# A gated recurrence and a local-attention network on one core: the convolution's taps and the input gate move to PSUM, the squares into the recurrence's tile, and the order is planned anew

## The chip, the cores and the metric

The kernel runs on one core of a Trainium2 chip. The metric is the device time of one execution in microseconds; of several executions the median is given. A core has five queues that run side by side: TensorE (PE, matrix products; its weight loads are shown apart as PEld), VectorE (DVE), ScalarE (ACT), GpSimd (POOL) and SyncE (SP, which only issues transfers here). Data lie in SBUF, products arrive in PSUM. All data are 32-bit floats but for two small constants.

## The reference

Input x is 16 sequences of 512 tokens with 128 channels. Each is normalised (xn), and goes through two branches whose results are multiplied and added to x.

```python
x = L0_attn_x
xn = _layernorm(x, axis=-1)
s = _L0_attn_ref(xn, ...)
g = _silu(_L0_ffn_ref(xn, ...))
x = x + s * g
```

The first branch is the one that the change touches. Its core:

```python
x_conv = _causal_depthwise_conv(x, conv_w, conv_b)      # four taps
r_t = jax.nn.sigmoid(x_conv @ W_r.T + b_r)
i_t = jax.nn.sigmoid(x_conv @ W_i.T + b_i)
a_t = a_base[None, None, :] ** (8.0 * r_t)
inp = i_t * x_conv
scale = jnp.sqrt(jnp.clip(1.0 - a_t * a_t, 0.0))
...
h = a * h + b                                           # over the tokens, b = scale * inp
...
out = out @ W_out.T
rms = jax.lax.rsqrt(jnp.mean(out * out, axis=-1, keepdims=True) + EPS)
return out * rms * gamma
```

The second branch is two layers of local attention (8 heads of 64, windows of 64 tokens that also see the window before; queries and keys are normalised, scaled and rotated) and a gated feed-forward of 341 hidden channels, each with a residual.

## The kernel before

**Tasks and a plan.** The kernel is not written as a loop. `all_work` lists every piece of work as a task: its name, its item (the sequence s, or layer and 128-token tile), its engine, an assumed duration in ns, a due time (`base`, in sequences), the tasks that it comes after, and the tiles that it opens and touches. `schedule` is a list scheduler: it holds assumed times for the five engines, for seven PSUM banks (`BANKS`; the norms have one of their own), each of 128 x 512 numbers, and for each kind of SBUF tile, of which `ROOM` says how many there are. Among the tasks that could start within `REACH` of the earliest, each engine takes the one with the smallest key, and the key is the due time in thousandths plus `TAU[name]`. So `TAU`, one number for each of some 110 task names, sets the order of the instructions in every queue. A change of the form of PE's tiles between neighbouring products (whole array, halves by row or column, quarters) has its assumed price. At the end the tasks are issued in that order, and each engine works its queue in order, waiting only for data and for tiles to come free.

**The task names.** For sequence s, the gates: `ld` loads, `fbn`, `fag`, `fpw`, `fnm` are the first layer norm, `ftx` transposes, `xp` copies to SBUF with room for the convolution's past, `xs0` and `xs1` feed the second branch. `c0` to `c3` are the four taps of the convolution on DVE (`taps`, L594, lines 600 to 604). For the first three sequences (`early`) two of the taps are products on PE instead (`cv`, L590) that `c3` adds. `gr` and `gi` are the gates' products, `sr` and `si` their tanh on ACT (`curve`, L609), `ea` the decay's exponential, `a2`, `m`, `rt` the root, `in` the gated input on DVE (L618), `u` its product with the root on POOL, `sc` the recurrence as one scan on DVE (L905), `yo` the output product, `s2` its squares on ACT (L906), `ms` their sum over channels on DVE (L639), `mp` the inverse root on POOL, `ss` the scaled output on DVE.

For each layer and tile of 128 tokens: `Q`, `K`, `V` are products; on DVE `rq1`, `rq2` (L669, L672) and the same for k multiply by the rotary tables straight from PSUM, and `addq`, `addk` (L676) add the two halves on POOL. ACT squares q and k, `red` (L681) sums the squares on DVE, `n0` to `n9` (L688 to L708) are an inverse root for a pair of tiles in small DVE steps, and `nrm` (L713, POOL) multiplies q and k by it. `tr` (L734, PE) transposes them, ACT copies them out, `sim` (L767, L773) are the scores, `nmA`, `nmB`, `exA`, `exB`, `rA`, `rB`, `PA`, `PB` the softmax (L779, L786, L794, L800), `PT` (L808) transposes the weights, `PV` (L820) mixes the values, `wo` (L838) projects. The feed-forward has `0g`, `0a`, `0ge`, `0hi` (L862), `0yy` and their like for layer 1. `matmul` (L578) is the helper of all large products, so its line stands for many tasks; the tile names in the profile (q, k, v, r, i, 0g, ...) tell them apart.

**Where the pieces lie.** Before, the taps read the padded input in SBUF and add in place to the tile `xc`, in SBUF too. The tanh of both gates goes from PSUM to SBUF (`thr`, `thi`), and `in` works in place on `thi`. The squares have a tile of their own, `s2`. What `u` (POOL) reads stays in SBUF in both kernels.

Of the kernel before, what the change touches and what calls it, by code (L numbers as in the profile page):

```python
# [12 lines left out]
AF = mybir.ActivationFunctionType  # L13
ALU = mybir.AluOpType
AX = mybir.AxisListType
PSUM = bass.MemoryType.PSUM

P = 128
# [6 lines left out]
KCH = 3  # L25
MASKED = -1e30
FIRST_STEP = 0.703952253
ROOT_SCALE = 0.375 * FIRST_STEP
# [6 lines left out]
    "0mv": 4, "1mv": 4, "fmv": 3, "g": 2, "gelu": 3, "h": 1, "hT": 2, "hid": 3, "kT": 4, "lx": 1, "max": 8,  # L35
    "ms": 3, "nx": 2, "oT": 2, "pT": 2, "pr": 3, "qT": 2, "rot": 4, "s": 4, "s2": 1, "sq": 2, "sw": 4, "th": 3,
    "thi": 2, "thr": 2, "vl": 4, "vs": 5, "x": 1, "xS": 5, "xc": 2, "xn0": 1, "xn1": 1, "xnf": 1, "xp": 2,
    "xtok": 2, "y": 3,
}

TAU = {
    "0a": 1332, "0ag": 1361, "0bn": -214, "0g": 295, "0ge": 1013, "0hT": 673, "0hi": -1180, "0nm": 2443,
    "0pw": 1629, "0r0": 999, "0r1": 4747, "0th": 1552, "0tx": 2339, "0yy": 3374, "1a": 1327, "1ag": 2191,
    "1bn": 1403, "1g": -1411, "1ge": -977, "1hT": 340, "1hi": 1571, "1nm": 2027, "1pw": 2179, "1r0": 3590,
    "1r1": -686, "1th": 4228, "1tx": 1647, "1yy": 1623, "K": 726, "PA": 1584, "PB": 1940, "PT": 417, "PV": 4109,
    "Q": 505, "TA": 1016, "TE": -162, "TR": 1100, "V": 1754, "a2": 4566, "addk": 1519, "addq": 648, "c0": 1400,
    "c1": 3192, "c2": 1035, "c3": 1776, "cv": 2050, "ea": 2438, "exA": 5954, "exB": 3760, "fag": -923, "fbn": 3289,
    "fnm": 1563, "fpw": 2230, "ftx": 2290, "gelu": 1287, "gi": 4289, "gr": 410, "in": -183, "kc0": 1034,
    "kc1": 2098, "kz": -827, "ld": 1054, "m": 2, "mp": -177, "ms": 763, "n0": -979, "n1": 1600, "n2": 1473,
    "n3": -1340, "n4": -1193, "n5": -1274, "n6": 1556, "n7": -75, "n8": -378, "n9": 3101, "nmA": 796, "nmB": -228,  # L50
    "nrm": 1410, "oT": 2811, "ot": 1591, "pT0": -1116, "pT1": 484, "qc0": 1520, "qc1": 1632, "rA": 1038, "rB": 714,
    "red": 3396, "rk1": -2269, "rk2": -1499, "rq1": 1107, "rq2": 1278, "rt": 2358, "s2": 1049, "sc": 3858,
    "si": -1114, "sim": -1210, "sqk": 2151, "sqq": 2061, "sr": 1587, "ss": 3359, "tf": -389, "tn": -1187,
    "tr": 103, "u": -1111, "vc": 3977, "vd": 1290, "vz": 3543, "wo": 3209, "xld": 1123, "xp": 1259, "xs0": 2257,
    "xs1": 3783, "y": 2584, "yo": 4491, "z": 1426, "zs": 1146, "zx": 2697,
}
# [4 lines left out]
SWITCH = (110, 115, 100, 97)  # L61
WHOLE, ROWS, QUARTERS, COLUMNS, EITHER = range(5)
TOGETHER = 1
RELOAD = 1450
# [34 lines left out]

def all_work(B, NT, lag=2, lead=1, vdve=(), early=3):  # L100
    w = Work()
# [8 lines left out]
    def gates(s):  # L110
        b = s - lead
        add("ld", s, "SP", 60, b, opens=[("xtok", s)], late=3500)
        ln("f", s, b, ("xtok", s), [("ld", s)])
        add("ftx", s, "PE", 440, b, [("fnm", s)], mode=WHOLE, opens=[("bank", "fx", s), ("xp", s), ("xS", s)], touches=[("xnf", s)])
        add("xp", s, "ACT", 480, b, [("ftx", s)], touches=[("xp", s), ("bank", "fx", s)])
        add("xs0", s, "ACT", 480, b, [("ftx", s)], touches=[("xS", s), ("bank", "fx", s)])
        add("xs1", s, "POOL", 1050, b, [("xp", s), ("xs0", s)], touches=[("xp", s), ("xS", s)])
        add("c0", s, "DVE", 800, b, [("xp", s)], opens=[("xc", s)], touches=[("xp", s)])
        on_pe = s < early
        for k in (1,) if on_pe else (1, 2, 3):  # L120
            add(f"c{k}", s, "DVE", 1100, b, [(f"c{k-1}", s)], touches=[("xp", s), ("xc", s)])
        if on_pe:
            add("cv", s, "PE", 1714, b, [("xp", s)], opens=[("bank", "cv", s)], touches=[("xp", s)])
            add("c3", s, "DVE", 670, b, [("c1", s), ("cv", s)], touches=[("bank", "cv", s), ("xc", s)])
        for g, t in (("r", "tr_"), ("i", "ti_")):
            add("g" + g, s, "PE", 857, b, [("c3", s)], opens=[("bank", g, s), ("th" + g, s)], touches=[("xc", s)])
            add("s" + g, s, "ACT", 600, b, [("g" + g, s)], touches=[("bank", g, s), ("th" + g, s)], table=EXP | GELU)
        add("ea", s, "ACT", 620, b, [("sr", s)], touches=[("thr", s)], table=EXP)
        add("in", s, "DVE", 670, b, [("si", s)], touches=[("thi", s), ("xc", s)])
        add("a2", s, "POOL", 1250, b, [("ea", s)], touches=[("thr", s)], opens=[("g", s)])  # L130
        add("m", s, "DVE", 340, b, [("a2", s)], touches=[("g", s)])
        add("rt", s, "ACT", 600, b, [("m", s)], touches=[("g", s)], table=ROOT)
        add("u", s, "POOL", 1250, b, [("rt", s), ("in", s)], touches=[("g", s), ("thi", s)])
        add("sc", s, "DVE", 1930, b, [("u", s)], touches=[("thr", s), ("thi", s)], opens=[("h", s)])
        add("yo", s, "PE", 872, b, [("sc", s)], touches=[("h", s)], opens=[("bank", "yo", s), ("s2", s), ("s", s)])
        add("s2", s, "ACT", 480, b, [("yo", s)], touches=[("bank", "yo", s), ("s2", s)])
        add("ms", s, "DVE", 620, b, [("s2", s)], touches=[("s2", s)], opens=[("ms", s)])
        add("mp", s, "POOL", 1255, b, [("ms", s)], touches=[("ms", s)])
        add("ss", s, "DVE", 1060, b, [("mp", s)], touches=[("ms", s), ("bank", "yo", s), ("s", s)])

    def attention(l, m):
# [26 lines left out]
        for j, n in enumerate(T):  # L168
            B_ = lambda nm, *k: ("bank", nm, *n, *k)
            one = n[1] % NT == 0  # L170
            before = (l, n[1] - 1)
            add("nrm", n, "POOL", 1950, b + j / 4, [("n9", M), ("addq", n), ("addk", n)], touches=[("y", *M), ("rot", *n)])
            if j == 0:
# [8 lines left out]
            for h in "AB":  # L182
                add("nm" + h, n, "DVE", 603, b + j / 4, [("sim", n)], touches=[B_("s" + h)], opens=[("max", *n, h)])
                add("ex" + h, n, "ACT", 1380, b + j / 4, [("nm" + h, n)], touches=[B_("s" + h), ("max", *n, h), ("pr", *n)], table=EXP)
                add("r" + h, n, "DVE", 95, b + j / 4, [("ex" + h, n)], touches=[("pr", *n)])
                add("P" + h, n, "POOL", 1035, b + j / 4, [("r" + h, n)], touches=[("pr", *n)])
            add("PT", n, "PE", 546, b + j / 4, [("PA", n), ("PB", n)], opens=[B_("p0"), B_("p1"), ("pT", *n)], touches=[("pr", *n)], mode=ROWS)
# [194 lines left out]
def gated_recurrence_kernel(ctx: ExitStack, tc: tile.TileContext, a: dict, out: bass.AP):  # L382
# [108 lines left out]
    def cast_masks():  # L491
# [15 lines left out]
    shapes = {  # L507
        "xtok": [P, NT, D], "xc": [P, L], "thr": [P, L], "thi": [P, L], "g": [P, L], "h": [P, L], "s2": [P, NT, D],
        "ms": [P, NT], "s": [P, NT, D], "rot": [P, 2, HEADS, DH], "sq": [P, 2, INNER], "sw": [P, HEADS, DH],
# [84 lines left out]
    def taps(s, i):  # L594

        v, xc = at["xp", s], at["xc", s]
        k = (i + 2) % 4
        v, w = v[:, k : k + L], c["cols"][:, k : k + 1]
        if i == 0:
            nc.vector.tensor_scalar(xc, v, w, c["conv_b"], ALU.mult, ALU.add)  # L600
        elif ("bank", "cv", s) in at and i == 3:
            nc.vector.tensor_tensor(xc, at["bank", "cv", s], xc, ALU.add)
        else:
            nc.vector.scalar_tensor_tensor(xc, v, w, xc, ALU.mult, ALU.add)

    def curve(s, g):

        i = "ri".index(g)
        nc.scalar.activation(at["th" + g, s], at["bank", g, s], AF.Tanh, scale=0.5, bias=half_b[:, i : i + 1])  # L609

# [5 lines left out]
    def gated(s):  # L616
        t = at["thi", s]
        nc.vector.scalar_tensor_tensor(t, t, 1.0, at["xc", s], ALU.add, ALU.mult)  # L618

# [16 lines left out]
    def mean_square(s, i):  # L636
        ms = at["ms", s]
        if i == 0:
            nc.vector.tensor_reduce(ms, at["s2", s], AX.X, ALU.add)  # L639
            return  # L640
        nc.gpsimd.tensor_scalar(ms, ms, 1.0 / D, 1e-6, ALU.mult, ALU.add)
        nc.gpsimd.tensor_tensor(ms, ms, mhalf[:, 0:NT], ALU.pow)
# [248 lines left out]
    def store(s):  # L891
# [13 lines left out]
        "sc": lambda s: nc.vector.tensor_tensor_scan(at["h", s], at["thr", s], at["thi", s], 0.0, ALU.mult, ALU.add),  # L905
        "yo": recurrent, "s2": lambda s: nc.scalar.activation(at["s2", s], tok(at["bank", "yo", s]), AF.Square),  # L906
        "ms": lambda s: mean_square(s, 0), "mp": lambda s: mean_square(s, 1), "ss": scaled,
# [111 lines left out]
```

## Time and profile before

| | |
|---|---|
| median of 3 runs | 1363.07 us (1361.11 to 1366.63) |
| profiled execution, its time | 1364.39 us |
| profiled execution, first to last instruction (span) | 1362.6 us |
| mean granted TensorE clock | 0.98 |
| busy: PE, DVE, ACT, POOL | 1287.0, 1131.4, 1152.6, 1069.5 us |
| busiest DVE group: `red` (L681) | 155.7 us, 128 of 1216 ns |
| taps on DVE (L604) | 65.0 us, 42 of 1547 ns |
| first tap (L600) | 10.3 us, 16 of 641 ns |
| gated input (L618) | 11.6 us, 16 of 728 ns |
| tanh of the input gate, of the other (L609) | 13.1 us, 11.1 us, 16 each |
| squares (L906), their sum (L639) | 9.9 us, 11.0 us, 16 each |
| table loads on ACT | 53 of 1283 ns |

The span is counted on the trace of one execution; busy times overlap between engines, and an engine's idle time costs only where PE, the fullest, waits for it. DVE's mean of 1547 ns for a tap hides two kinds of taps, which the range of durations shows.

### The profile page before, as it was taken

To read this page: it belongs to the slowest core of one execution; us is meant where nothing else is said; L and a number is where in the kernel's file an instruction comes from. 1 tells how busy PE (TensorE), PEld (TensorE's weight loads), DVE (VectorE), ACT (ScalarE), POOL (GpSimd) and SP (SyncE) were. 2 spreads that over 40 slices of the span, in tenths; PEclk is the share of its full clock that TensorE was granted. 3 is DMA by queue.
4 is the path that set the end of the run, shared out by engine and by line. 5 is a ranking of instruction groups with operands and counts; after the bars stand their busy time and mean duration, and the time that the engine had idled before them with its cause. 6 is when DMAs were issued, how large, how long until landed. Compare 5 with 4: busy or idle time off the path is not lost.

```text
span 1362.6 us, 43814 instructions
## 1 busy us (share of the span) xinstructions
PE 1287.0 (94%) x17162; PEld 724.3 (53%) x17162; DVE 1131.4 (83%) x2752; ACT 1152.6 (85%) x3703; POOL 1069.5 (78%) x1009
## 2 busy tenths in 40 slices
PE   6689899999999999999999999999999999999985
PEld 2355456555555555555555555555455555656453
DVE  6888889888998888899898988989888888877752
ACT  5698899888899888899888889988888898889672
POOL 6796989697896878889797988978788787868461
PEclk9799999999999999999999999999999999999988
DMA  6011011111111101111111111111111110112100
GB/s 199 5 45 30 16 23 28 28 41 33 37 33 28 48 18 49 32 37 33 29 37 29 49 33 37 33 29 29 28 37 37 29 33 25 34 29 58 28 21 24
DMA packets 46766, 49.43 MB, mean 36 GB/s; under 512 B 4704, under 2 KB 31456, under 8 KB 46560
## 3 DMA queue, kind: packets, MB, share of 16 engines
q1 hardware_dynamic: 46560, 46.63, 13.7%
q8 instruction: 136, 2.23, 0.7%
q14 instruction: 70, 0.57, 0.1%
HBM read 13.05 MB, written 4.19 MB: 13 GB/s over the span
## 4 chain that ended last, share of the span: by engine, by line
PE 66%; DVE 18%; issue 5%; ACT 5%; POOL 5%; DMA 0%; POOLq 0%; DVEq 0%; ACTq 0%
PE q L578 6%; PE k L578 6%; PE sA L773 5%; PE v L578 5%; PE o L820 5%; PE x L838 4%; PE t L734 4%; DVE norms L681 3%; PE p L808 3%; PE 0g L578 3%; PE 0y L578 3%; PE 0a L578 3%; PE 1a L578 3%; PE 1g L578 3%; DVE sw L672 3%
## 5 line engine op out<-in xcount | busy, mean ns | idle before, releaser
L676 POOL TENSOR_TENSOR rot<-rot,sw 128x512 f32<-128x512 f32 x256 | 326.8, 1283 | 79.3 <-DVE sw L672 68.1
L800 POOL TENSOR_TENSOR pr<-pr,sum 128x512 f32<-128x512 f32 x256 | 267.0, 1052 | 95.1 <-DVE sum L794 89.9
L713 POOL TENSOR_TENSOR rot<-rot,y 128x1024 f32<-128x1024 f32 x128 | 268.2, 2118 | 18.3 <-DVE y L708 18.2
L786 ACT ACTIVATE pr<-sB,max 128x128 f32<-128x128 f32 x512 | 187.4, 423 | 8.6 <-DVE max L779 7.3
L786 ACT ACTIVATE pr<-sA,max 128x128 f32<-128x128 f32 x512 | 192.1, 467 | 0.0
L681 DVE TENSOR_REDUCE norms<-sq 128x16 f32<-128x1024 f32 x128 | 155.7, 1216 | 3.7 <-ACT sq L662 1.3
L811 ACT COPY pT<-p 128x512 f32<-128x512 f32 x256 | 144.2, 658 | 8.1 <-PE p L808 8.1
L786 ACT ACTIVATION_READ_ACCUMULATOR pr<-sA,max 128x1 f32 x512 | 150.7, 306 | 0.0
L669 DVE TENSOR_TENSOR rot<-q,table 128x512 f32<-128x512 f32 x128 | 87.5, 684 | 57.6 <-PE q L578 36.1
L578 PE MATMUL q<-wqkv,xS 128*64 128x512 f32 (+1 forms) x502 | 134.2, 618 | 0.2 <-ACT pr L786 0.2
L773 PE MATMUL sA<-kT,qT 64*64 64x128 f32 x2048 | 133.9, 270 | 0.0
L773 PE MATMUL sB<-kT,qT 64*64 64x128 f32 x2048 | 133.6, 270 | 0.0
L578 PE MATMUL k<-wqkv,xS 128*64 128x512 f32 (+1 forms) x476 | 132.2, 601 | 0.4 <-ACT pr L786 0.3
L743 ACT COPY kT<-t 128x256 f32<-128x256 f32 x256 | 100.6, 434 | 34.9 <-PE t L734 34.4
L820 PE MATMUL o<-pT,vl 128*64 128x64 f32 x2048 | 128.3, 226 | 0.9 <-ACT pT L811 0.9
L786 ACT ACTIVATION_READ_ACCUMULATOR pr<-sB,max 128x1 f32 x512 | 128.2, 261 | 0.0
L578 PE MATMUL v<-wqkv,xS 128*64 128x512 f32 (+1 forms) x500 | 127.2, 603 | 0.7 <-ACT pr L786 0.7
L820 PE MATMUL o<-pT,vs 128*64 128x64 f32 x2048 | 125.7, 224 | 0.2
L838 PE MATMUL x<-oT,wo 128*64 128x257 f32 x1024 | 122.7, 381 | 2.8 <-ACT oT L828 2.3
L773 PEld LDWEIGHTS sA<-kT,qT 64*64 64x64 f32 x2048 | 120.3, 133 | 9.2 <-issue 0.2
L820 PEld LDWEIGHTS o<-pT,vl 128*64 128x64 f32 x2048 | 107.1, 139 | 31.7 <-ACT pT L811 12.2
L773 PEld LDWEIGHTS sB<-kT,qT 64*64 64x64 f32 x2048 | 120.2, 133 | 0.0
(152 smaller groups left out, 3195.7 us busy)
## 6 DMA issues: line engine op xcount, KB each, us to landing
vl<-vs SPq DMA_DIRECT2D x224, 128.0 KB, 2.3
xtok<-in_x SPq DMA_DIRECT2D x16, 256.0 KB, 3.2
x<-in_x SPq DMA_DIRECT2D x16, 256.0 KB, 3.1
out<-th SPq DMA_DIRECT2D x16, 256.0 KB, 2.3
wqkv<-in_wqkv SPq DMA_DIRECT2D x2, 768.0 KB, 7.1
w<-in_w SPq DMA_DIRECT2D x2, 384.0 KB, 6.6
rot<-in_rope SPq DMA_DIRECT2D x1, 512.0 KB, 6.2
wo<-in_wo SPq DMA_DIRECT2D x2, 256.0 KB, 5.3
```

The costliest lines, as they stand in the source:

```text
L578: nc.tensor.matmul(ps[col : col + step], w[:, col : col + step], v, start=start, stop=stop)
L669: nc.vector.tensor_tensor(at["rot", *n][:, i], src, tab, ALU.mult)
L676: nc.gpsimd.tensor_tensor(r, r, at["sw", *n, "qk"[i]], ALU.add)
L681: nc.vector.tensor_reduce(at["nx", *pair(n)][:, 0, 16 * j : 16 * j + 16], sq, AX.X, ALU.add)
L713: nc.gpsimd.tensor_tensor(flat, flat, bc(at["y", *pair(n)][:, 0, 16 * j : 16 * j + 16], DH), ALU.mult)
L743: nc.scalar.copy(at["kT", *pair(n)][:, :, col : col + 64], four(at["bank", f"t{w}", *n])[:, 1])
L773: nc.tensor.matmul(out_(w, par)[:, p, :], q[r, p, half[w]], k[r, p, col : col + P], start=False, stop=p == 3)
L786: nc.scalar.activation(at["pr", *n][:, g, :], sim[:, p, :], AF.Exp, bias=at["max", *n, h][:, p : p + 1], accum_out=at["sum", *n][:, g : g ...
L800: nc.gpsimd.tensor_tensor(w, w, bc(at["sum", *n][:, g], P), ALU.mult)
L811: nc.scalar.copy(at["pT", *n][:, w], heads(at["bank", f"p{w}", *n]))
L820: nc.tensor.matmul(o[64 * par : 64 * par + 64, p, 64 * w : 64 * w + 64], at[("vl", "vs")[w], *n][:, h * DH : (h + 1) * DH], pT[:, w, 4 * p ...
L838: nc.tensor.matmul(ps[64 * r : 64 * r + 64, 0 : 2 * P + 1], w, o[:, k, 1 - r : 2 * P + 2 - r], start=k == 0, stop=k == 3)
```

## The change

The changed parts are these. (1) From the fourth sequence on, the taps are summed in a PSUM bank: `c0` opens it, `c1` and `c2` add in place, `c3` reads it and writes `xc` in SBUF. In the first three sequences `c0` writes `xc`, `c1` adds its tap in place to the bank that holds PE's two taps, and `c3` adds bank and `xc`. (2) The input gate's tanh is written in place in its bank; `in` reads it from there and opens `thi`. (3) The squares go to the tile `h`, whose contents the output product has read by then; `s2` as a tile is gone. (4) The assumed durations of some tasks are changed, all of `TAU` is replaced, and two constants are named: `EARLY`, 3 as before, and `SKEW`, which is 0 and so adds nothing.

```diff
-    "ms": 3, "nx": 2, "oT": 2, "pT": 2, "pr": 3, "qT": 2, "rot": 4, "s": 4, "s2": 1, "sq": 2, "sw": 4, "th": 3,
...
+    "ms": 3, "nx": 2, "oT": 2, "pT": 2, "pr": 3, "qT": 2, "rot": 4, "s": 4, "sq": 2, "sw": 4, "th": 3, "thi": 2,
...
-    "0a": 1332, "0ag": 1361, "0bn": -214, "0g": 295, "0ge": 1013, "0hT": 673, "0hi": -1180, "0nm": 2443,
...
+    "0a": -186, "0ag": 4568, "0bn": 2786, "0g": 1865, "0ge": 1058, "0hT": -1527, "0hi": -1865, "0nm": -2283,
...
-        add("c0", s, "DVE", 800, b, [("xp", s)], opens=[("xc", s)], touches=[("xp", s)])
-        on_pe = s < early
-        for k in (1,) if on_pe else (1, 2, 3):
-            add(f"c{k}", s, "DVE", 1100, b, [(f"c{k-1}", s)], touches=[("xp", s), ("xc", s)])
+        b += round(SKEW * (B - 1 - s) / max(B - 1, 1), 3)
+        on_pe, C = s < early, ("bank", "cv", s)
         if on_pe:
-            add("cv", s, "PE", 1714, b, [("xp", s)], opens=[("bank", "cv", s)], touches=[("xp", s)])
-            add("c3", s, "DVE", 670, b, [("c1", s), ("cv", s)], touches=[("bank", "cv", s), ("xc", s)])
-        for g, t in (("r", "tr_"), ("i", "ti_")):
-            add("g" + g, s, "PE", 857, b, [("c3", s)], opens=[("bank", g, s), ("th" + g, s)], touches=[("xc", s)])
-            add("s" + g, s, "ACT", 600, b, [("g" + g, s)], touches=[("bank", g, s), ("th" + g, s)], table=EXP | GELU)
+            add("c0", s, "DVE", 700, b, [("xp", s)], opens=[("xc", s)], touches=[("xp", s)])
+            add("cv", s, "PE", 1714, b, [("xp", s)], opens=[C], touches=[("xp", s)])
+            add("c1", s, "DVE", 660, b, [("cv", s)], touches=[("xp", s), C])
+            add("c3", s, "DVE", 660, b, [("c0", s), ("c1", s)], touches=[C, ("xc", s)])
+        else:
+            add("c0", s, "DVE", 600, b, [("xp", s)], opens=[C], touches=[("xp", s)])
+            for k in (1, 2, 3):
+                add(f"c{k}", s, "DVE", 660, b, [(f"c{k-1}", s)], opens=[("xc", s)] if k == 3 else [], touches=[("xp", s), C])
+        for g in "ri":
+            add("g" + g, s, "PE", 857, b, [("c3", s)], opens=[("bank", g, s)] + [("thr", s)] * (g == "r"), touches=[("xc", s)])
+            add("s" + g, s, "ACT", 600, b, [("g" + g, s)], touches=[("bank", g, s)] + [("thr", s)] * (g == "r"), table=EXP | GELU)
...
-        add("in", s, "DVE", 670, b, [("si", s)], touches=[("thi", s), ("xc", s)])
+        add("in", s, "DVE", 660, b, [("si", s)], opens=[("thi", s)], touches=[("bank", "i", s), ("xc", s)])
...
-        add("s2", s, "ACT", 480, b, [("yo", s)], touches=[("bank", "yo", s), ("s2", s)])
-        add("ms", s, "DVE", 620, b, [("s2", s)], touches=[("s2", s)], opens=[("ms", s)])
+        add("s2", s, "ACT", 480, b, [("yo", s)], touches=[("bank", "yo", s), ("h", s)])
+        add("ms", s, "DVE", 600, b, [("s2", s)], touches=[("h", s)], opens=[("ms", s)])
...
-            add("nrm", n, "POOL", 1950, b + j / 4, [("n9", M), ("addq", n), ("addk", n)], touches=[("y", *M), ("rot", *n)])
+            add("nrm", n, "POOL", 1880, b + j / 4, [("n9", M), ("addq", n), ("addk", n)], touches=[("y", *M), ("rot", *n)])
...
-                add("P" + h, n, "POOL", 1035, b + j / 4, [("r" + h, n)], touches=[("pr", *n)])
+                add("P" + h, n, "POOL", 1010, b + j / 4, [("r" + h, n)], touches=[("pr", *n)])
...
-        v, xc = at["xp", s], at["xc", s]
+        v, c_ps = at["xp", s], at["bank", "cv", s] if ("bank", "cv", s) in at else None
...
-            nc.vector.tensor_scalar(xc, v, w, c["conv_b"], ALU.mult, ALU.add)
-        elif ("bank", "cv", s) in at and i == 3:
-            nc.vector.tensor_tensor(xc, at["bank", "cv", s], xc, ALU.add)
+            nc.vector.tensor_scalar(at["xc", s] if ("xc", s) in at else c_ps, v, w, c["conv_b"], ALU.mult, ALU.add)
+        elif i == 3 and s < EARLY:
+            nc.vector.tensor_tensor(at["xc", s], c_ps, at["xc", s], ALU.add)
         else:
-            nc.vector.scalar_tensor_tensor(xc, v, w, xc, ALU.mult, ALU.add)
+            nc.vector.scalar_tensor_tensor(at["xc", s] if i == 3 else c_ps, v, w, c_ps, ALU.mult, ALU.add)
...
-        i = "ri".index(g)
-        nc.scalar.activation(at["th" + g, s], at["bank", g, s], AF.Tanh, scale=0.5, bias=half_b[:, i : i + 1])
+        i, ps = "ri".index(g), at["bank", g, s]
+        nc.scalar.activation(ps if i else at["thr", s], ps, AF.Tanh, scale=0.5, bias=half_b[:, i : i + 1])
...
-        t = at["thi", s]
-        nc.vector.scalar_tensor_tensor(t, t, 1.0, at["xc", s], ALU.add, ALU.mult)
+        nc.vector.scalar_tensor_tensor(at["thi", s], at["bank", "i", s], 1.0, at["xc", s], ALU.add, ALU.mult)
...
-            nc.vector.tensor_reduce(ms, at["s2", s], AX.X, ALU.add)
+            nc.vector.tensor_reduce(ms, tok(at["h", s]), AX.X, ALU.add)
...
-        "yo": recurrent, "s2": lambda s: nc.scalar.activation(at["s2", s], tok(at["bank", "yo", s]), AF.Square),
+        "yo": recurrent, "s2": lambda s: nc.scalar.activation(tok(at["h", s]), tok(at["bank", "yo", s]), AF.Square),
```

## The prediction

> **What bounds the kernel now.** I read the page's slices first, then TensorE's waits, then windows of 40 us, then the timelines of one stall.
>
> ```profile
> PE   6689899999999999999999999999999999999985
> ...
> PEclk9799999999999999999999999999999999999988
> ```
>
> Each digit is the busy share of 34 us, in tenths. TensorE (PE) is full from slice 6 to slice 38; only the edges have room. VectorE (83%), ScalarE (85%) and GpSimd (78%) matter only where they make PE wait. The view of PE's waits (what waited, for what: us in total, times, longest) says where that is:
>
> ```profile
> PE t L734 <- POOL rot L713: 25.5, 28, 1.1
> PE fx L568 <- ACT xnf L558: 12.1, 2, 11.6
> PE r L578 <- DVE xc L602: 6.7, 1, 6.7
> ```
>
> The second is the start (first load, first layer norm), the third a prologue wait. The first is the middle: 21.1 us of it, in 22 waits, lie between 160 and 1160 us. The windows show it as a beat (us, busy time of PE, PEld, DVE, ACT, POOL, then granted clock, DMA share, GB/s):
>
> ```profile
> 440.00:480.00 40.00, 38.09 (x556) 22.91 (x554) 36.14 (x105) 35.00 (x117) 35.00 (x35) 0.96 0.18 45
> ...
> 720.00:760.00 40.00, 40.00 (x508) 21.09 (x506) 33.41 (x61) 35.26 (x113) 30.71 (x27) 1.00 0.11 28
> 760.00:800.00 40.00, 38.09 (x579) 23.12 (x576) 37.42 (x112) 36.47 (x120) 36.17 (x36) 1.00 0.17 42
> ```
>
> A period (one sequence through everything) is two windows: 79.77 us from one "0g" group on PE to the next (639.41 to 719.17 us in the chain of waits). 1.9 us of it is idle. The timelines of POOL, DVE and PE at that place (start, length, idle before and releaser):
>
> ```profile
> 764.43 8.92 POOL L713 TENSOR_TENSOR rot<-rot,y 128x1024 f32<-128x1024 f32 x4 [0.89 <-DVE y L708]
> ```
>
> ```profile
> 764.36 3.05 DVE L604 SCALAR_TENSOR_TENSOR xc<-xp,cols,xc 128x512 f32<-128x512 f32 x2
> 767.33 0.41 DVE L845 TENSOR_TENSOR xS<-x,xS 128x257 f32<-128x257 f32 x1
> 767.67 2.05 DVE L604 SCALAR_TENSOR_TENSOR xc<-xp,cols,xc 128x512 f32<-128x512 f32 x1
> ```
>
> ```profile
> 766.92 0.71 PE L734 MATMUL t<-squares,rot 64*128 64x64 f32 x16 [0.81 <-POOL rot L713]
> 767.47 0.66 PE L808 MATMUL p<-squares,pr 64*128 64x64 f32 x16
> 769.22 0.71 PE L734 MATMUL t<-squares,rot 64*128 64x64 f32 x16 [1.10 <-POOL rot L713]
> ```
>
> PE waits twice for GpSimd's normalisations (L713), and these run beside exactly the three convolution taps (L604) that the change rewrites. Forms by line (duration min/median/max):
>
> ```profile
> L604 DVE SCALAR_TENSOR_TENSOR xc<-xp,cols,xc x42: 714/2050/2360, 16.1 to 1087.0; 128x512 f32<-128x512 f32 x42
> L862 DVE SCALAR_TENSOR_TENSOR hid<-0a,cols,gelu x48: 718/749/752, 109.0 to 1265.4; 128x512 f32<-128x512 f32 x48
> L713 POOL TENSOR_TENSOR rot<-rot,y x128: 1892/1905/2831, 43.4 to 1305.8; 128x1024 f32<-128x1024 f32 x128
> ```
>
> A tap reads two tensors in SBUF. Alone it takes 714 ns, beside GpSimd 2050 and more, and GpSimd stretches too: the first L713 here took 2.44 us against its median 1.905. The same operation with one tensor in PSUM (L862) never left 718 to 752 in 48 runs.
>
> **The taps.** From the fourth sequence on (13 sequences) c0 writes a bank, c1 and c2 read and write it, c3 reads it and writes SBUF. In-place PSUM at this size is not in the trace; the nearest row is L862, 749 ns, with a PSUM source. Bounds are 714 (the free tap) and 762 (L862 plus 13, by which small operations that write the norms in PSUM, L694 at 198, exceed those that write y in SBUF, L702 at 185); I take 749. Here the three taps took 0.74, 2.27 and 2.05, 5.06 us; then 3 x 0.749 = 2.25. c0 (L600, median 516 ns) loses its SBUF destination: between 516 and 750, taken 680 as for the PSUM-reading L669. DVE gains 2.81 - 0.16 = 2.65 us in each such period.
>
> [...]
>
> **What that gives PE, in the old order.** Without stretch L713 ends at 764.43 + 1.905 = 766.33 instead of 766.87, and the second at about 768.2 instead of 769.1 (back to back they follow at 1.87). The first transpose comes 0.5 us earlier; the second, behind the 0.55 of p, about 1.0 earlier. So 1.9 us of idle becomes 0.9. The long taps (two of 2.05 or more) recur in the steady periods, sequences 5 to 15, so 11 x 1.0 = 11 us. What is late next is the same L713, released by the inverse norm (y, L708), which is a chain on DVE and no longer helped by faster taps.
>
> **The clock.** Four periods are longer: "0g" starts at 397.02, 478.25, 559.64 and 639.41 us, so 81.23 and 81.39 where 79.77 is usual. In 2 us windows the clock falls to about 0.5 at 286 to 290, 446 to 452, 528 to 534 and 1088 to 1092 us. The two stalls lie 47.8 and 50.1 us behind a period's "0g" (766.92 and 769.22 less 719.17), so at 445 and 447, at 526 and 528: each drop follows that period's stalls. About 1.6 us each, four times: 6.3 us. Shorter stalls should spare them; bounds 0 and 6.3, taken 6.
>
> **The input gate.** si (L609) writes its bank in place, `in` (L618, 728 ns mean) reads it: 749 by L862, 16 x 0.02 = 0.3 us on DVE. ScalarE's row for si is 858 median to SBUF against 687 for sr; a PSUM destination lies between 687 and 858, worth 0 to 2.7 us on an engine with 15% free. Taken 0. The bank is let go after `in`, not after si: 718.14 + 0.86 to 719.52 + 0.69 in one period, 1.2 us later.
>
> **Squares in the recurrence's tile.** Same instructions (L906, L639), another address: nothing. h now lives until `ms`; with one h, the next scan waits for it. Scans are a period apart, scan to `ms` 6 us (1202.7 to 1208.8). Cover: 70 us.
>
> **Early sequences.** Three keep two taps on PE (12 matmuls either way). c1 no longer adds to xc but to the bank: it now waits for PE's `cv`, and behind it on DVE stands whatever is queued. Before, c1 took 0.77, 0.99 and 2.36 us; then 0.75 each, 1.9 us less on DVE. c3's 6.7 us wait at 43.12 starts with a GpSimd table and 0.69 + 0.99 + 0.69 of taps, so 0.3 us of it goes. Taken 0.
>
> **The new order.** All priorities change, on every queue, SP's loads too (DMA share 0.1 in the middle: nothing). PE's instructions stay the same in kind and number. I counted 34 changes of the matmul tiling per period; a group of 16 transposes alone takes 0.64 us to the next start (725.43 to 726.07), two together 1.14, so a change costs some 0.07 to 0.1 us, and three more or fewer move 13 periods by up to 4 us either way. The 1.0 us of idle that the old order would keep is what a new order can hide, since one group of q, k or v (0.86 us) put ahead of the transpose covers it: 11 x 0.9 = 10 us at most, taken 4. It can lose as much elsewhere; its cost bounds are those of the rivals.
>
> Sum against the profiled execution (span 1362.6, time 1364.4): 11 + 6 + 4 = 21, giving 1343.4. It lies 1.3 above the median of the runs, 1363.07; the forecast is 1342. Within this case: 1357 if nothing but half the stall goes, 1332 if all stalls and clock drops go (21.1 + 6.3 and 4 of tiling).
>
> **Rivals.**
> Also the edges: PE is idle 32 us before 160 us, of which 12 are the first load, and at clock 0.83 and 0.91 between 40 and 120 us (some 10 us). If the replan fills a third of both, 10 us, on top of the 31: 1322. For it: every engine has gaps there. Against: chains of one sequence set them.
> No change: the idle is an artefact of order and only moves. PE works 77.9 of 79.77 us; a stall of 1.9 in another place costs the same: 1363. For it: the inverse norm, not the tap, releases L713. Against: GpSimd gets 1.4 us back (8.92 to 7.5) just there.
> Slower, the bank: seven PSUM banks serve all of PE's groups, and c0 must find a free one, standing at the head of DVE's queue until it does. In the traced period c0 to c3 lasts from 760.43 to 769.72, 9.3 us; with the gate's 1.2 that is 10.5 us of one bank. A period has 7 x 79.77 = 558 bank-us, so 1.9% are gone. If banks are what paces PE, that is 1.5 us per period, 13 x 1.5 = 19 us, with the gain lost: 1382. It decides above about 1.6 us per period (21 / 13). [...] For it: PE's weight loads wait for bank readers (o for ACT's pT 12.9 us, v for ACT's pr 10.0). Against: PE itself lost 0.7 us to ACT's pr on v; and taps back to back hold a bank 2.9 us, a 0.5 us price, 7 us in all.
> That the change doesn't do what it says: c0 picks its target by whether xc is open yet, which holds from the fourth sequence on only until c3; I give this nothing of its own.
>
> **Chances.** Forecast 0.52, edges too 0.11, no change 0.10, slower 0.27: planned orders rest on assumed durations, so I don't trust the replan further than that. Half a per cent is about what a measurement tells from no change. Faster 0.63, same 0.10, slower 0.27. The range 1324 to 1384 takes in the bank's case and most of the edges'; the forecast's own is 1332 to 1357.
>
> **What would show it.** Taps of 714 to 762 ns with no long ones; L713 back at 1.9 us; t waiting for L713 under 12 us in total; clock 1.00 in the middle windows; a period near 78.5. Wrong if the period stays at 79.8 with PE waiting on ACT or DVE instead, if c0 shows idle time before it for a bank, or if the middle gains and the edges give it back.

## The result and the profile after

The changed kernel takes 1370.70 us (median of 8 runs, 1369.44 to 1372.20) beside 1365.26 us of the kernel before (8 runs, 1360.53 to 1366.83). The ratio is 1.0048 with a 95% interval of 1.0033 to 1.0063: slower by half a per cent, where 1.6% faster was forecast. The profiled execution has a span of 1370.3 us (before 1362.6). Executions of the kernel before spread from 1357.8 to 1367.7 us over all sessions, with granted clocks from 0.983 to 0.977, and their medians from 1360.5 to 1365.8, so ratios of different sessions can differ by some 0.4%.

The forms by line of the changed kernel (durations min/median/max) show that the operations did what they should:

```profile
L605 DVE TENSOR_SCALAR cv<-xp,cols x13: 783/802/806, 57.9 to 1091.9; 128x512 f32<-128x512 f32 x13
...
L609 DVE SCALAR_TENSOR_TENSOR cv<-xp,cols,cv x29: 733/754/756, 17.8 to 1093.7; 128x512 f32<-128x512 f32 x29
L609 DVE SCALAR_TENSOR_TENSOR xc<-xp,cols,cv x13: 747/748/748, 60.3 to 1094.5; 128x512 f32<-128x512 f32 x13
```

No tap of L609 takes 2 us any more; all lie between 733 and 756 ns. Only the first tap into a bank (`c0`, L605) costs more than assumed, 802 ns. VectorE's busy time fell from 1131.4 to 1107.6 us, GpSimd's from 1069.5 to 1047.5. Yet PE now waits elsewhere. The page's rows for PE and its clock, and the view of PE's waits (what waited, for what: us in total, times, longest):

```profile
PE   5889899999999999999999999999999999999985
...
PEclk9899999999999999999999999999999999999998
```

```profile
PE t L738 <- POOL rot L717: 17.9, 16, 1.6
PE fx L573 <- ACT xnf L563: 11.6, 1, 11.6
PE 0th L573 <- DVE xn L567: 6.8, 11, 0.6
PE i L583 <- DVE sum L798: 6.1, 9, 0.7
```

The wait for the normalisation is smaller in total (25.5 before), but it is one long one per period now, and two waits are new: 0.6 us for a layer norm (11 times) and 0.7 us of the input gate's product (9 times). The timelines of POOL, DVE and PE at the place that corresponds to the one shown of the kernel before:

```profile
683.21 7.48 POOL L717 TENSOR_TENSOR rot<-rot,y 128x1024 f32<-128x1024 f32 x4 [3.57 <-DVE y L712]
```

```profile
679.11 0.43 DVE L692 TENSOR_SCALAR norms<-norms 128x32 f32<-128x32 f32 x2
...
682.87 0.29 DVE L712 SCALAR_TENSOR_TENSOR y<-norms,y 128x32 f32<-128x32 f32 x2
683.08 0.80 DVE L605 TENSOR_SCALAR cv<-xp,cols 128x512 f32<-128x512 f32 x1
683.91 0.76 DVE L609 SCALAR_TENSOR_TENSOR cv<-xp,cols,cv 128x512 f32<-128x512 f32 x1
684.58 0.42 DVE L849 TENSOR_TENSOR xS<-x,xS 128x257 f32<-128x257 f32 x1
684.91 0.74 DVE L609 SCALAR_TENSOR_TENSOR cv<-xp,cols,cv 128x512 f32<-128x512 f32 x1
685.69 0.75 DVE L609 SCALAR_TENSOR_TENSOR xc<-xp,cols,cv 128x512 f32<-128x512 f32 x1
```

```profile
685.16 0.72 PE L738 MATMUL t<-squares,rot 64*128 64x64 f32 x16 [1.26 <-POOL rot L717]
686.59 1.08 PE L583 MATMUL i<-xc,squares 128*64 128x512 f32 x4 [0.71 <-DVE sum L798]
687.47 1.06 PE L583 MATMUL r<-xc,squares 128*64 128x512 f32 x4
```

The inverse norm (L692 to L712, two chains side by side) ends at 683.16. Four normalisations take 7.48 us beside four taps, where they took 8.92. But GpSimd stood idle for 3.57 us before them, waiting for that inverse norm, and PE arrives at the transpose 1.26 us too early all the same. Then it runs into the gate's products, which the new order puts right behind the last tap: the tap ends at 686.44, `i` starts at 686.59. (The view names the reciprocal next in DVE's queue as releaser; `i` reads xc, whose last tap ends just ahead of it.) Before, only `r` followed the last tap, and `i` came 27 us later (769.87 and 796.82 us in that trace).

From one layer-norm product of layer 0 to the next (0th on PE), ten steady periods last 820.8 us here (306.6 to 1127.4), 82.1 each, against 802.6 us, 80.3 each, before. A period is 81.11 us, or 82.7 in the six of the ten in which PE falls to half clock for 3.4 us about the end of the second wait (a clock episode in what follows); before, it was 79.77, or 81.2 to 81.6 with an episode.

### The profile page after: what moved, and what is told of

The parts are those of the page before. It is cut to its first block, busy times and chain, and to the rows that moved or that the text cites. A ratio compares the mean times of both kernels' runs of the same rounds, so it can differ in the third digit from the quotient of the medians.

```text
span 1370.3 us, 43462 instructions
## 1 busy us (share of the span) xinstructions
PE 1292.5 (94%) x16894; PEld 729.3 (53%) x16894; DVE 1107.6 (81%) x2752; ACT 1154.9 (84%) x3703; POOL 1047.5 (76%) x1009
## 4 chain that ended last, share of the span: by engine, by line
PE 49%; DVE 22%; ACT 20%; issue 4%; POOL 4%; DMA 0%; POOLq 0%; ACTq 0%; DVEq 0%
ACT pr L790 10%; PE q L583 5%; DVE norms L685 5%; PE o L824 4%; PE t L738 3%; PE k L583 3%; ACT sq L666 3%; PE 1a L583 3%; PE sA L777 3%; PE 0y L583 3%; PE 1y L583 3%; PE 1g L583 3%; PE 0g L583 3%; PE 0a L583 3%; POOL rot L717 3%
## 5 line engine op out<-in xcount | busy, mean ns | idle before, releaser
L717 POOL TENSOR_TENSOR rot<-rot,y 128x1024 f32<-128x1024 f32 x128 | 253.0, 1996 | 49.5 <-DVE y L712 49.5
L790 ACT ACTIVATE pr<-sB,max 128x128 f32<-128x128 f32 x512 | 183.7, 400 | 23.2 <-DVE max L783 21.0
L790 ACT ACTIVATE pr<-sA,max 128x128 f32<-128x128 f32 x512 | 187.0, 431 | 0.0
L790 ACT ACTIVATION_READ_ACCUMULATOR pr<-sA,max 128x1 f32 x512 | 137.4, 271 | 0.0
L583 PE MATMUL k<-wqkv,xS 128*64 128x512 f32 (+1 forms) x498 | 129.2, 603 | 1.2 <-ACT pr L790 1.2
L790 ACT ACTIVATION_READ_ACCUMULATOR pr<-sB,max 128x1 f32 x512 | 121.8, 239 | 0.0
L738 PEld LDWEIGHTS t<-squares,rot 64*128 64x128 f32 x2048 | 75.0, 140 | 71.9 <-POOL rot L717 33.4
```

The costliest lines, as they stand in the source:

```text
L583: nc.tensor.matmul(ps[col : col + step], w[:, col : col + step], v, start=start, stop=stop)
L717: nc.gpsimd.tensor_tensor(flat, flat, bc(at["y", *pair(n)][:, 0, 16 * j : 16 * j + 16], DH), ALU.mult)
L738: nc.tensor.transpose(four(at["bank", f"t{w}", *n])[:, i, p, :], r[rows, i, 2 * p : 2 * p + 2, :], c["ident"][rows, rows])
L790: nc.scalar.activation(at["pr", *n][:, g, :], sim[:, p, :], AF.Exp, bias=at["max", *n, h][:, p : p + 1], accum_out=at["sum", *n][:, g : g ...
```

## The experiments

In each of them the order of every queue is fixed: the plan of one of the two kernels is made first, each queue's list of tasks is taken from it, and the scheduler may only take the next task of that list, so that it does no more than give out the banks. Comments in the code excerpts are added here. Ratios are to the kernel before, run on the same chip. In the traces PE's groups come in the same order in the kernel before and in both old-order runs that move no product, and where nothing is moved a fixed order lasts as long as the plan it copies: 79.88 and 89.61 us from the second to the fourth `0th` in the last new-order run below, 79.87 and 89.59 in the changed kernel.

### The new operations in the old order

```diff
-    order = schedule(work, TAU, ROOM)
+    other = all_work_other(B, NT)                  # the tasks of the kernel before
+    fixed = sequences(other, schedule(other, TAU_OTHER, ROOM_OTHER))
+    order = schedule(work, TAU_OTHER, ROOM, fixed)
```

> All new operations (taps and input gate in PSUM, squares in h), but every queue's order is that of the kernel before. Theory A (the operations gain, the new order loses): 12 to 21 us under the kernel before, so about 1345 to 1353; GpSimd's four normalisations in a row 7.5 us instead of 8.9, the transposes' wait for them 1 us per period instead of 1.9, fewer half-clock episodes. Theory B (the bank that the taps hold slows PE): 1365 or more, up to 1382, with PE or its weight loads waiting on readers of banks. Theory C (the taps don't matter to PE at all, only the order does): within 3 us of the kernel before.

Measured: 1346.16 us against 1360.53, ratio 0.9888 (0.9873 to 0.9903). Its timelines of POOL and PE at the same place:

```profile
673.18 7.49 POOL L917 TENSOR_TENSOR rot<-rot,y 128x1024 f32<-128x1024 f32 x4 [1.36 <-DVE y L912]
```

```profile
675.14 0.71 PE L938 MATMUL t<-squares,rot 64*128 64x64 f32 x16 [0.54 <-POOL rot L917]
...
677.00 0.71 PE L938 MATMUL t<-squares,rot 64*128 64x64 f32 x16 [0.66 <-POOL rot L917]
```

The two waits of 0.81 and 1.10 us are now 0.54 and 0.66; in all, PE waits 17.3 us for the normalisations where it waited 25.5:

```profile
PE t L938 <- POOL rot L917: 17.3, 28, 1.1
```

The clock, too, is full in the middle (windows: us, busy of PE, PEld, DVE, ACT, POOL, clock, DMA share, GB/s); each steady period is 79.06 to 79.08 us, none is longer:

```profile
640.00:680.00 40.00, 38.80 (x576) 23.01 (x574) 32.59 (x80) 35.77 (x116) 29.18 (x27) 1.00 0.14 38
680.00:720.00 40.00, 40.00 (x522) 21.95 (x517) 36.48 (x94) 35.78 (x117) 36.85 (x37) 1.00 0.16 37
720.00:760.00 40.00, 38.81 (x564) 22.41 (x563) 32.62 (x81) 36.25 (x117) 29.12 (x28) 1.00 0.12 33
```

Theory A holds; the bank (theory B) falls, since here the taps hold a bank for 6.7 us (668.93 to 675.64) and PE is faster, and so does theory C. So the operations win 1.1%, and the new order loses 1.6% (1.0048 / 0.9888 = 1.016; without the reference, 1370.70 / 1346.16, it is 1.8%).

### The new order with taps in SBUF

```diff
-            add("c0", ..., opens=[C], touches=[("xp", s)])
+            add("c0", ..., opens=[("xc", s)], touches=[("xp", s)])
...
-            nc.vector.scalar_tensor_tensor(at["xc", s] if i == 3 else c_ps, v, w, c_ps, ALU.mult, ALU.add)
+            to = at["xc", s] if s >= EARLY else c_ps
+            nc.vector.scalar_tensor_tensor(to, v, w, to, ALU.mult, ALU.add)
```

> The changed kernel in its own order, but from the fourth sequence on the taps are summed in SBUF again. Theory A: slower than the changed kernel by 5 to 20 us (1376 to 1390), since the taps again lie beside GpSimd's normalisations and stretch them. Theory B: faster than the changed kernel, under 1368. Theory C: within 3 us of 1371.

Measured: 1429.05 us, ratio 1.0495 (1.0479 to 1.0511), some 4.4% above the changed kernel. Theory A had the sign, but the size was far above its 20 us. The taps' form and PE at that place say why:

```profile
L812 DVE SCALAR_TENSOR_TENSOR xc<-xp,cols,xc x39: 741/2051/2292, 56.3 to 1146.1; 128x512 f32<-128x512 f32 x39
```

```profile
792.34 0.71 PE L941 MATMUL t<-squares,rot 64*128 64x64 f32 x16 [1.55 <-POOL rot L920]
797.59 1.98 PE L785 MATMUL i<-xc,squares 128*64 128x512 f32 x4 [4.54 <-DVE sum L1001]
```

What was 0.71 us before `i` is 4.54, 3.8 us more, close to the 3 x 1.3 us by which the three taps are longer; and `i` itself takes 1.98 us in place of 1.08, at half clock. The new order leaves no slack between the last tap and the gates' products: it is an order for short taps only, and with long ones it costs PE nearly their full excess and a clock episode in every one of the ten periods (6.8 us or more each, between 359 and 1154 us).

### Only the taps, in the old order

The kernel before in its own order; c0 to c2 of the fourth and later sequences write the bank, all else is as before.

```diff
-        v, xc = at["xp", s], at["xc", s]
+        v, xc = at["xp", s], at["xc", s] if ("xc", s) in at else at["bank", "cv", s]
...
-            nc.vector.scalar_tensor_tensor(xc, v, w, xc, ALU.mult, ALU.add)
+            nc.vector.scalar_tensor_tensor(xc, v, w, xc if s < 3 else at["bank", "cv", s], ALU.mult, ALU.add)
```

> The kernel before in its own order, only the taps of the fourth and later sequences summed in PSUM; gate, squares and early sequences as before. Theory A: within 3 us of the run with all new operations in the old order, since the gate and the squares are worth nothing. If the bank held by the input gate costs something, this is faster than that run by more than 3 us. Theory C: as the kernel before.

Measured: 1347.36 us, ratio 0.9896 (0.9880 to 0.9913), 1.2 us from the run with all operations and inside its interval. The gate in PSUM, the squares in h and the early taps are worth nothing that these runs can tell.

### One product moved in the old order

The task list of PE is edited in 11 periods. One more buffer of rot is needed, since the query's tile is opened ahead of the transpose that frees one; a th buffer makes room for it.

```diff
-    "rot": 4, ... "th": 3,
+    "rot": 5, ... "th": 2,
...
+    q = fixed[0]                                    # PE's list
+    for k in [k for k, t in enumerate(q) if t[0] == "gr"]:
+        if [t[0] for t in q[k - 4 : k + 2]] == ["PV", "tr", "PT", "tr", "gr", "Q"]:
+            q.insert(k - 3, q.pop(k + 1))           # Q ahead of the first tr
```

> The new operations in the old order, and in 11 periods the first query product is put ahead of the two transposes that still wait 1.2 us per period; one more buffer for rot so that it may start, one less for th. If a wait of PE is worth its length: up to 0.86 us in each of 11 periods, 4 to 9 us under the old-order run without the edit, ratio to the kernel before about 0.982 to 0.986. If the wait only moves (the query's bank or its readers come later): ratio 0.988 to 0.991, as without the edit.

Measured: 1331.31 us against 1364.15, ratio 0.9779 (0.9748 to 0.9810), the best of all, and more than the 4 to 9 us that were expected. PE's wait for the normalisation in this run:

```profile
PE t L942 <- POOL rot L921: 9.3, 18, 1.1
```

It is 9.3 us in all (17.3 without the edit), 0.4 per period in the middle where it was 1.2; a period is 78.10 us, 0.97 less than 79.07. Ten of them give 9.7 us of the 14 us between the two profiled spans (1344.1 and 1330.1). Another 4.7 lie ahead of the fourth `0th` (302.9 against 307.5 us), and only 1.2 of these in an edited period. The other 3.4 come where nothing was moved, by the traces mostly from the fifth rot buffer: in the old-order run without the edit DVE finds none free at the start, until GpSimd has read the raw rotary table out of one (`table`, L694).

```profile
35.62 0.69 DVE L873 TENSOR_TENSOR rot<-q,table 128x512 f32<-128x512 f32 x1 [5.00 <-POOL table L694]
```

With five buffers DVE does not wait there, and PE's wait for the first sequences' taps (`r`) falls from 5.8 to 2.0 us. No run has the buffers without the moved product, so the two are told apart by their places in the traces alone.

### One product moved in the new order, at two places

Ahead of the transpose (with the same two buffers changed):

```diff
+    q = fixed[0]
+    for k in [k for k, t in enumerate(q) if t[0] == "gi"]:
+        if [t[0] for t in q[k - 1 : k + 3]] == ["tr", "gi", "gr", "Q"]:
+            q.insert(k - 1, q.pop(k + 2))           # Q ahead of tr
```

> The changed kernel in its own order, but in 10 periods (the seventh to the last sequence) the query product that follows the gates' products is put ahead of the transpose that waits 1.26 us; one more rot buffer, one less th. Theory D (what the new order loses is this one place: 2.0 us of waits per period, and the half-clock episode that follows it in every second period, 0.8 us per period): 0.9 to 1.7 us less per period, 9 to 17 us under the changed kernel, ratio to the kernel before 0.992 to 0.998. Theory E (the loss is spread over tiling changes, banks and smaller waits, so that the moved product only shifts a wait): within 4 us of the changed kernel, ratio 1.002 to 1.008.

Or between the transpose and the gates' products (buffers as in the changed kernel):

```diff
-            q.insert(k - 1, q.pop(k + 2))
+            q.insert(k, q.pop(k + 2))               # tr, Q, gi, gr
```

> The changed kernel in its own order, but in the same 10 periods the query product stands between the transpose and the gates' products, so that it covers the 0.71 us wait for the last tap. No buffer is changed. Theory D: 0.7 us per period and at least half of the clock episodes go, 7 to 15 us under the changed kernel, ratio 0.994 to 1.000. Theory E: within 4 us of the changed kernel, ratio 1.002 to 1.008.

Measured: 1356.48 us, ratio 0.9953 (0.9933 to 0.9974) for the first, 1351.88 us, ratio 0.9927 (0.9896 to 0.9957) for the second; the changed kernel stands at 1.0048. The second edit's place in its trace:

```profile
673.62 0.71 PE L944 MATMUL t<-squares,rot 64*128 64x64 f32 x16 [1.27 <-POOL rot L923]
674.26 1.08 PE L789 MATMUL q<-wqkv,xS 128*64 128x512 f32 x4
675.17 1.03 PE L789 MATMUL i<-xc,squares 128*64 128x512 f32 x4
```

So one group of four instructions, moved over two other groups in 10 periods, gives back 1.2% of the 1.6% that the new order loses, somewhat more than theory D gave it: the ten periods last 804.2 us in place of 820.8. Both edits remove every clock episode between 160 and 1290 us, and the period becomes 80.76 us or 80.35 us where it was 81.11 or 82.7 (in three of the ten, after the second edit, 80.5 to 80.7). The second gains more though its PE still waits 1.27 us at the transpose: the 0.71 us behind it are gone. The first keeps both waits, at 0.43 and 0.71 us, and no episode follows them. What is left between 80.35 and the old order's 79.07 us is spread: 1.9 us of waits per period against 1.2, and three more changes of the tiling.

### The moved product without the taps

The kernel before with its own operations, and the same edit of PE's list as in the old-order run above. The buffers are rot 5, th 2 and, other than there, one less of vs (4).

> The kernel before, with all its own operations (taps in SBUF), and only the edit of the order: the first query product ahead of the two transposes in 11 periods (one more rot buffer, one less of th and of vs). If the gain of the best run comes from the edit alone: as that run, ratio 0.975 to 0.981. If taps and edit each give their part: the edit covers 0.86 of the 1.9 us of waits and ends the four half-clock episodes, 0.9 x 11 + 6 = 16 us, ratio 0.985 to 0.992. If the taps must be short first for the edit to work (the normalisations stretched by the taps then end later still): within 4 us of the kernel before, 0.997 to 1.003.

Measured: 1344.44 us, ratio 0.9851 (0.9823 to 0.9879). PE's wait for the normalisation:

```profile
PE t L938 <- POOL rot L917: 12.2, 17, 1.1
```

The edit with its buffers is worth 1.5%, the operations alone 1.1%, both together 2.2%. The ten steady periods leave out the start, and with it what the fifth rot buffer gives there: 802.6 us before, 787.8 with the edit, 790.7 with the operations, 781.0 with both, so gains of 14.7, 11.9 and 21.5 us. Each gives a part. They overlap in the wait that both shorten (25.5 us before, then 12.2, 17.3 and 9.3 in the whole run) and in the clock: the three episodes of these periods, about 4.8 us, are gone with either.

## Why the prediction failed

**What was right.** The place (PE's transposes waiting for GpSimd's normalisation), the cause (taps and normalisations stretching each other), the taps at 749 ns (measured 733 to 756), the four normalisations at 7.5 us (7.48 and 7.49). For the operations in the old order the sum said 11 us of waits and 6 of clock, 17; measured are 15 us (0.0112 x 1364), of which the profiles show 8.2 in the waits (25.5 to 17.3) and four episodes of about 1.6. The number of episodes is in part luck: executions of the kernel before had more or fewer of them, by their clocks of 0.977 to 0.983. The waits shrank by 0.7 us per period, not 1.0: `c0` with its bank costs 781 to 814 ns in that run, above its bounds of 516 to 750, and in the old order it stands inside the chain of the inverse norm that releases the normalisation. GpSimd was idle 1.36 us there instead of 0.89, and 0.26 of the difference is `c0` (0.78 for 0.52 us).

**The step that failed** is "The new order": "11 x 0.9 = 10 us at most, taken 4", a gain. It was a loss of some 22 us ((1.0048 - 0.9888) x 1363), larger than the gain of the operations. I named it as able to lose "as much elsewhere", but took a small gain because one product could cover the wait. No such product covered the wait in the old order, and none does in the new; that a cover exists (it does, 0.97 us per period in the old order) doesn't mean that a plan uses it. The loss, from the two profiled executions, changed kernel and old-order run, over the ten steady periods (820.8 against 790.7 us, 30.1 more; start and end give 4 back, so that 26 are left between the spans, where the ratios of two sessions say 22): waits of 2.6 against 1.2 us per period, 14 us; a half-clock episode in six of the ten periods, about 1.6 each, 10 us; three more tiling changes per period, 2 to 3 us by the prediction's price; some 3 us are not accounted for.

**Why the plan puts PE there too early** is argued, not shown. The scheduler assumes 108 ns for a step of the inverse norm and 120 between dependent ones, so about 2.3 us for ten steps; in the trace above the ten steps of the two chains take 4.05 us (679.11 to 683.16). The assumed taps became right with the change (660 assumed, 750 measured, in place of 1100 beside 2050), and what releases the normalisations is this chain. But the old plan rests on the same assumed steps, and no run plans anew with longer ones, so the cause within the planner stays open.

**The rivals.** The slower case came out, but not for its reason. The bank was not what paces PE: no first tap waited for one, the 6.7 us hold in the old-order run cost nothing visible, and the changed kernel's hold is 3.4 us. "No change: the idle only moves" described the mechanism best, with its price too low: the idle moved, grew by 0.7 us in a usual period, and took the clock with it. The first sequences, which I thought could gain, are level with the old-order run (the fourth 0th at 306.6 against 307.5 us).

**PSUM against SBUF.** In the changed kernel the taps with an operand in PSUM take 733 to 756 ns, where the fastest one in SBUF took 714 before; `c0` into its bank takes 802 ns against 516 (medians). The taps won 13 us in the old order all the same (1347.36 against 1360.53 us).

## What to carry to other kernels

Where a change brings a new planned order with it, price the two apart: run the new operations in the old order of every queue, and the other way round if it can be done. In a kernel whose fullest engine leaves 1.9 us in 80, a wait of under a microsecond behind another one is worth looking for on the chip, because half clock may come with it (in six of the ten periods of the changed kernel, with 0.71 to 0.90 us behind 1.09 to 1.27). A single neighbouring product moved into it was worth as much as the rewrite of the operations (14.7 against 11.9 us in ten periods). When such a move needs another buffer, look in the trace where the buffer itself gains.

## What the runs showed of the hardware

**When the clock falls.** The waits of PE in one period of the middle, and how often a clock episode came with them, in the one traced execution of each:

| run | waits, us | episodes |
|---|---|---|
| new operations, old order | 0.54 and 0.66, within 2.4 us | 0 of 11 periods |
| kernel before | 0.81 and 1.10, within 3.1 us | 4 of 11 |
| changed kernel | 1.26 and 0.71, within 2.7 us | 6 of 10 |
| new order, query between | one, 1.1 to 1.65 | 0 of 10 |
| new order, query ahead | 0.43 and 0.71 | 0 of 10 |
| new order, taps in SBUF | 1.55 and 4.54 | 10 of 10 |

So equal waits do not always come with one: in the changed kernel 1.26 or 1.27 and 0.71 or 0.72 us came with an episode in five periods and without one in three. An episode lasts 3.4 us and costs about 1.6; in the last row it lasts 6.8 us or more. In the changed kernel episodes begin at 358.0, 439.9, 603.7, 767.5, 931.4 and 1095.2 us, from the second on 163.8 apart, which is one long and one short period (82.7 + 81.1). There and in the kernel before they begin between 0.2 us ahead of the end of the second wait and 0.7 us behind it, and the two waits of these periods are 1.90 to 2.05 us together, with products between them. What picks one of two periods with the same waits, no run shows.

One episode, in windows of 2 us with PE's busy time first and the clock third from the end:

```profile
602.00:604.00 2.00, 0.81 (x18) 0.71 (x20) 1.97 (x6) 1.25 (x4) 2.00 (x2) 0.93 0.46 99
604.00:606.00 2.00, 2.00 (x6) 0.73 (x8) 0.88 (x8) 0.46 (x3) 2.00 (x2) 0.50 0.19 39
606.00:608.00 2.00, 2.00 (x8) 0.43 (x4) 0.69 (x1) 1.17 (x2) 2.00 (x3) 0.72 0.01 1
```

PE is busy for 0.81 of 2 us, and the next window is at half clock throughout, in which PE counts as fully busy: half-clock time hides in the busy time.

**A first tap into PSUM** costs 783 to 806 ns in the changed kernel, where the same operation into SBUF took 516 at its median before, while a tap with one operand in PSUM takes 733 to 756 ns with its result there and 747 or 748 with it in SBUF.
